# Cross-attention with two key sets: the third group's exponentials row by row

## The chip, the cores and the metric

The kernel runs on one core of a Trainium2 chip. The metric is the device time of one execution in microseconds (us). Five engines work side by side, each through its own queue in program order: TensorE (matrix products, PE in the profile, with PEld for its weight loads), VectorE (DVE), ScalarE (ACT), GpSimd (POOL) and SyncE (SP), which issues nearly all transfers between the device memory and the on-chip memory. All arithmetic is in 32-bit floats.

## The reference, cut to what matters

Two batches of 2048 tokens with 640 channels attend, with 20 heads of 32 channels, to 154 context rows of 1024 channels. The first 77 rows are text and the other 77 are a second set with its own key and value weights. There are two softmaxes per token and head, one over each set of 77 keys, and their outputs are added.

```python
def _attend(q, k, v, sm_scale):
    scores = jnp.einsum('bhsd,bhld->bhsl', q, k) * sm_scale
    probs = jax.nn.softmax(scores, axis=-1)
    return jnp.einsum('bhsl,bhld->bhsd', probs, v)
...
text = encoder_hidden_states[:, :TEXT_LEN, :]      # 77 rows
ip = encoder_hidden_states[:, TEXT_LEN:, :]        # 77 rows
q = _split_heads(hidden_states @ Wq.T, H)
k = _split_heads(text @ Wk.T, H)
v = _split_heads(text @ Wv.T, H)
out_text = _merge_heads(_attend(q, k, v, sm_scale))
k_ip = _split_heads(ip @ Wk_ip.T, H)
v_ip = _split_heads(ip @ Wv_ip.T, H)
out_ip = _merge_heads(_attend(q, k_ip, v_ip, sm_scale))
out = out_text + IP_SCALE * out_ip                 # IP_SCALE = 1
out = out @ Wo.T + bo
return out + residual
```

## The kernel before

Channels are cut into five chunks of 128, which are four heads each. A step u (0 to 19) is one batch, one chunk and one half (1024 tokens) of the sequence; `step_of` gives them. Two steps with the same batch and chunk make a pair q (0 to 9). The 1024 tokens of a step are eight tiles of 128, and `GROUPS` cuts these into three groups s of three, three and two tiles. A group holds, for each token on its partition, four heads with two rows of 77 scores per tile: 24 rows in the first and second groups, 16 rows (1232 numbers on a partition) in the third.

The order of all work is one list of words, `SCHEDULE`, written out by hand and emitted word by word. Each engine takes its own instructions in that order. The words that matter here, with s the group and u the step:

- `q.u.h@bank`: TensorE computes the queries of half h into one of eight accumulator banks (`queries`, L191); `cq.u.h`: ScalarE scales and copies them out (`take_queries`, L201).
- `Rs.u@half`: TensorE computes the scores into four banks, one for each head (`scores`, L223); `Ks.u`: ScalarE copies them to the buffer `pb` in four copies (`take`, L235).
- `Ms.u`: VectorE takes the maximum of each row (`maxima`, L261); `Ss.u`: GpSimd subtracts it, over the whole group (`subtract`, L275); `Es.u`: ScalarE takes the exponential in place, over the whole group (`exponential`, L281).
- `Ds.u`: VectorE sums the rows and takes the reciprocals (`sums`, L288 and L290); `Ns.u`: GpSimd multiplies by them (`normalise`, L295); `Ts.u`: VectorE transposes blocks of 32 x 32 (`transpose`, L302).
- `A.q@half`: TensorE multiplies both steps of a pair with the values (`attend`, L311), which needs all six transposes of the pair; `CA.q`: ScalarE copies the result out (`take_attention`, L334 and L338).
- `k` and `v` project keys and values (L132), and `ck` and `cv` are ScalarE's copies of them (L673 and L675; the first two of the keys at L548). `m`, `o` and `p` are products of the output projection, and `cm` and `co` add them up on VectorE (L467, L502, L508). `LX` loads tokens, `VS` spreads the values over partitions (L148).

After the last pair a finishing part (from L789, names `F`, `Y`, `X`, `V`) does the second batch's output projection. A word waits, through semaphores, for the words that write what it reads and for those that still read what it writes; the eight banks are used in turn, so that a product can start only when ScalarE or VectorE has emptied its bank. A function for exponentials row by row is there already (`exponential_of`), but the table `DIRECT` that selects it is empty.

Of the kernel before, what the change touches and what calls it, by code (L numbers as in the profile page):

```python
# [9 lines left out]
F32 = mybir.dt.float32  # L10
AF = mybir.ActivationFunctionType
ALU = mybir.AluOpType
AX = mybir.AxisListType

B, S, C, CC, LT = 2, 2048, 640, 1024, 154
# [5 lines left out]
def kernel(  # L21
# [25 lines left out]
    nc = tc.nc  # L47
    P = 128
    NC = C // P
    NCC = CC // P  # L50
    G = P // D
# [7 lines left out]
    L = TEXT  # L59
# [1 line left out]
    NK = (2 * L + D - 1) // D  # L61
    LP = NK * D
    SCALE = 1.0 / float(D) ** 0.5
    DIRECT = {}
    NP = B * NC
    NU = NP * SUB
    OPEN = 4
# [4 lines left out]
    small = ctx.enter_context(tc.tile_pool(name="small", bufs=4))  # L72
# [67 lines left out]
    def square_v(c):  # L140
        for b in range(B):
            nc.vector.transpose(squares(b * NC + c), vT[:, b])

    def spread_v(q, half):

        for g in range(G * half // 2, G * (half + 1) // 2):
            for r in range(G):
                nc.sync.dma_start(  # L148
                    out=v4s[q % 2][r * D : (r + 1) * D, g].rearrange("p k d -> p (k d)"),
                    in_=squares(q)[g * D : (g + 1) * D],  # L150
                )
# [28 lines left out]
    def load_wq(q):  # L180
        c = q % NC
        nc.sync.dma_start(
            out=wqs[q % 3], in_=WqT[:, ts(c, P)].rearrange("(k p) o -> p k o", p=P)
        )
# [25 lines left out]
    def keys_of(u, s):  # L210
        return pb_of(u, s)[:, :, :, : 2 * L]

    def rows_of(u, s):
        return keys_of(u, s).rearrange("p n g (t l) -> p (n g) t l", l=L)

    def scores(u, s, ps):

        _, b, c, _ = step_of(u)
        first, n = GROUPS[s]
        for t in range(n):  # L220
            h, st = divmod(first + t, TB // P)
            for g in range(G):
                nc.tensor.matmul(  # L223
                    ps[g][:, ts(t, 2 * L)],
                    qTs[(u, h)][g * D : (g + 1) * D, ts(st, P)],
                    kT[g * D : (g + 1) * D, c, b].rearrange("p t l -> p (t l)"),
                    start=True,
                    stop=True,
                )

    def take(u, s, ps):

        n = GROUPS[s][1]
        for g in range(G):
            nc.scalar.copy(  # L235
                keys_of(u, s)[:, :, g], ps[g][:, : n * 2 * L].rearrange("p (n l) -> p n l", n=n)
            )
# [3 lines left out]
    def rows_in(ps, n):  # L241
        return ps[:, : n * 2 * L].rearrange("p (n t l) -> p n t l", n=n, t=2)

    def exponential_of(u, s, ps):

        n = GROUPS[s][1]
        for g in range(G):
            for t in range(n):
                for x in range(2):
                    nc.scalar.activation(  # L250
                        rows_of(u, s)[:, t * G + g, x],
                        rows_in(ps[g], n)[:, t, x],
                        AF.Exp,
                        bias=maxs[(u, s)][:, t * G + g, x : x + 1],
                    )

    def maxima(u, s, ps=None):
        n = GROUPS[s][1] * G
        mx = small.tile([P, n, 2], F32, tag=f"mx{n}", name=f"mx_{u}_{s}")
        if ps is None:  # L260
            nc.vector.tensor_reduce(mx, rows_of(u, s), AX.X, ALU.max)  # L261
        else:
            for g in range(G):
                nc.vector.tensor_reduce(
                    mx.rearrange("p (n g) t -> p g n t", g=G)[:, g],
                    rows_in(ps[g], n // G),
                    AX.X,
                    ALU.max,
                    negate=True,
                )  # L270
        maxs[(u, s)] = mx
# [11 lines left out]
    rdens = {}  # L283

    def sums(u, s):
        n = GROUPS[s][1] * G
        den = small.tile([P, n, 2], F32, tag=f"den{n}", name=f"den_{u}_{s}")
        nc.vector.tensor_reduce(den, rows_of(u, s), AX.X, ALU.add)  # L288
        rden = small.tile([P, n, 2], F32, tag=f"rden{n}", name=f"rden_{u}_{s}")
        nc.vector.reciprocal(rden, den)  # L290
        rdens[(u, s)] = rden

    def normalise(u, s):
        n = GROUPS[s][1] * G
        nc.gpsimd.tensor_tensor(  # L295
            rows_of(u, s), rows_of(u, s), rdens[(u, s)].unsqueeze(3).to_broadcast([P, n, 2, L]), ALU.mult
        )

    def transpose(u, s):
# [4 lines left out]
    def attend(q, pa):  # L304

        zones = pb[:, ds(q % 2, SUB)].rearrange("p z n g (k s) -> p (z n) g k s", k=NK)
        for k in range(NK):
            for r in range(G):
                rows = slice(r * D, (r + 1) * D)
                for g in range(G):  # L310
                    nc.tensor.matmul(  # L311
                        pa[r][g * D : (g + 1) * D, :],
                        v4s[q % 2][rows, g, k, :],
                        zones[rows, :, g, k, :],
                        start=(k == 0),
                        stop=(k == NK - 1),
                    )
# [10 lines left out]
    def take_attention(q, pa):  # L328
        b, c = divmod(q, NC)
        rows = rows_of_attention(b, c).rearrange("p i (n r s) -> p r i n s", n=NT // NH, r=G)  # L330
        for r in range(G):
            tokens = pa[r].rearrange("p (i n s) -> p i n s", i=NHB, n=NT // NH)
            if q % 2 == 0:
                nc.scalar.copy(rows[:, r], tokens)  # L334
                continue

            for sub in range(SUB):
                nc.scalar.copy(rows[:, r, ts(sub, NH)], tokens[:, ts(1 - sub, NH)])  # L338
# [204 lines left out]
    for t in range(2):  # L543

        ps = halves[t][G - 2 + t]
# [76 lines left out]
    def emit(word):  # L622
        name, _, where = word.partition("@")
        k, *args = name.split(".")
        x, y = (*(int(a) for a in args if a.isdigit()), None, None)[:2]
        i = int(k[1:]) if k[1:].isdigit() else None
        if k[0] == "R":
            at[name] = halves[int(where)]
            scores(x, i, at[name])
        elif k == "A":  # L630
            at[name] = halves[int(where)]
            attend(x, at[name])
        elif k == "CA":
            take_attention(x, at[f"A.{x}"])
        elif k == "SQ":
            square_v(x)
        elif k == "VS":
            spread_v(x, y)
        elif k == "LX":
            load_block(x, y)  # L640
        elif k == "LQ":
            load_wq(x)
        elif k == "LK":
            load_w(x)
        elif k == "LO":
            load_wo()
        elif k == "LF":
            for part in PARTS:
                fetch(0, part)
        elif k[0] in "KMSEDNT":  # L650
            ps = at[f"R{i}.{x}"]
            if k[0] == "K":
                take(x, i, ps)
            elif k[0] in "ME":
                direct = (x, i) in DIRECT
                if k[0] == "M":
                    maxima(x, i, ps if direct else None)
                elif direct:
                    exponential_of(x, i, ps)
                else:  # L660
                    exponential(x, i)
            else:
                dict(S=subtract, D=sums, N=normalise, T=transpose)[k[0]](x, i)
        elif k == "q":
            at[name] = banks[int(where)]
            queries(x, y, at[name])
        elif k == "cq":
            take_queries(x, y, at[name[1:]])
        elif k in ("k", "v"):
            at[name] = banks[int(where)]  # L670
            project_kv(4 * x + 2 * (k == "v") + y, at[name])
        elif k == "ck":
            nc.scalar.copy(kT[:, x, :, y, :], keys_in(at[name[1:]]))  # L673
        elif k == "cv":
            nc.scalar.copy(vT[:, :, ds(y * L, L)], keys_in(at[name[1:]]))  # L675
        elif k in ("o", "p"):
            at[name] = banks[int(where)]
            last_chunk(at[name], int(k == "p"), x, range(NC - (k == "p")))
        elif k == "co":
            store_last(at[name[1:]], 0, x)  # L680
        elif k[0] == "m":
            at[name] = banks[int(where)] if where else at[f"m{JOINS[i]}.{x}"]
            product(i, 0, x, at[name])
        elif k[:2] == "cm":
            take_product(int(k[2:]), 0, x, at[name[1:]])
        elif k[0] == "W":
            sum_w(i)
        elif k[0] == "G":
            sum_t(i, 0, x)
        else:  # L690
            finish(k, args, where)
# [152 lines left out]
    for word in SCHEDULE:  # L844
        emit(word)
# [32 lines left out]
```

## Time and profile before

| | us | of the span |
|---|---|---|
| median of 2 runs (509.55 and 509.91) | 509.73 | |
| span of the profiled execution, first to last instruction | 509.3 | |
| TensorE busy with products | 496.4 | 97% |
| VectorE busy | 431.5 | 85% |
| GpSimd busy | 414.3 | 81% |
| ScalarE busy | 242.8 | 48% |
| subtractions of all groups on GpSimd (L275, 60) | 175.6 | |
| exponentials of all groups on ScalarE (L281, 60) | 94.9 | |

The profile has no time for the execution other than its span, which stands 0.4 us below the median of the runs. An engine's busy time leaves out register, branch and semaphore instructions. TensorE's products overlap each other, so its busy time is from the first to the last of a stretch without a pause. In a timeline, a row gives the start, the time it took, the engine, the line in the kernel, the operation, what it writes and reads with shapes, how many alike stand in it, and in brackets how long the engine had been idle and what ended that.

### The profile page before, as it was taken

What the parts mean: (1) busy time and instruction counts of PE and PEld (TensorE: products, weight loads), DVE (VectorE), ACT (ScalarE), POOL (GpSimd) and SP (SyncE); (2) the same over time, 40 slices, a digit from 0 to 9 for tenths busy, and PEclk for the clock granted to TensorE, in tenths of its full rate; (3) what the DMA queues carried; (4) which work ended last, traced back from release to release, by engine and by line L of the source; (5) the groups of instructions that cost most, each with busy time, mean ns of one, the idle gap of its engine ahead of it and who ended that gap; (6) DMA issues with size and microseconds to landing.
All of it is one profiled execution on the core that took longest, in us unless ns stands there. A gap on an engine that the chain in (4) does not pass through costs nothing.

```text
span 509.3 us, 9862 instructions
## 1 busy us (share of the span) xinstructions
PE 496.4 (97%) x4114; PEld 292.1 (57%) x4114; DVE 431.5 (85%) x401; ACT 242.8 (48%) x423; POOL 414.3 (81%) x176
## 2 busy tenths in 40 slices
PE   9999999999989999999999999996999999999996
PEld 5657557557458556446655565553666576444442
DVE  0078989989987989977995999799299999999986
ACT  1266657577566567654636544663466453100000
POOL 0078999999997979988998899799399999468750
PEclk9999999999999999999999999997999999999999
DMA  8994050502441554577444724534914022310017
GB/s 272 357 287 134 16 136 11 142 3 71 129 148 42 157 192 141 200 238 250 146 134 146 242 62 155 210 106 134 322 30 124 27 82 64 125 62 1 21 62 268
DMA packets 67468, 69.34 MB, mean 136 GB/s; under 512 B 5472, under 2 KB 47200, under 8 KB 67424
## 3 DMA queue, kind: packets, MB, share of 16 engines
q1 hardware_dynamic: 66704, 68.00, 42.5%
q8 instruction: 32, 0.52, 0.4%
q10 hardware_dynamic: 720, 0.72, 0.4%
q14 instruction: 12, 0.10, 0.1%
HBM read 54.94 MB, written 10.49 MB: 128 GB/s over the span
## 4 chain that ended last, share of the span: by engine, by line
PE 69%; DVE 9%; DMA 8%; POOL 8%; ACT 2%; SPq 2%; issue 1%; DVEq 0%; POOLq 0%
PE bank L191 22%; PE bank L835 11%; PE bank L477 8%; PE bank L223 8%; PE bank L311 6%; PE bank L132 6%; POOL pb L275 5%; PE bank L457 4%; DMA x<-in_x_dram 3%; DVE pb L302 3%; POOL pb L295 3%; PE bank L487 2%; DVE mx L261 2%; DVE den L288 2%; DMA wo_ct<-in_L_xattn_Wo_dram 2%; DMA aT<-in_L_xattn_Wk_ip_dram 2%
## 5 line engine op out<-in xcount | busy, mean ns | idle before, releaser
L275 POOL TENSOR_TENSOR pb<-pb,mx 128x1848 f32<-128x1848 f32 (+1 forms) x60 | 175.6, 2946 | 42.4 <-DVE mx L261 42.3
L295 POOL TENSOR_TENSOR pb<-pb,rden 128x1848 f32<-128x1848 f32 (+1 forms) x60 | 175.6, 2948 | 15.4 <-DVE rden L290 15.1
L191 PE MATMUL bank<-x,wq 128*128 128x512 f32 x400 | 182.5, 606 | 4.8 <-DMA x<-in_x_dram 4.5
L261 DVE TENSOR_REDUCE mx<-pb 128x24 f32<-128x1848 f32 (+1 forms) x60 | 109.3, 1837 | 34.4 <-ACT pb L235 34.4
L191 PEld LDWEIGHTS bank<-x,wq 128*128 128x128 f32 x400 | 75.0, 193 | 92.8 <-issue 82.8
L235 ACT COPY pb<-bank 128x462 f32<-128x462 f32 (+1 forms) x240 | 101.9, 534 | 54.2 <-PE bank L223 53.6
L281 ACT ACTIVATE pb<-pb 128x1848 f32<-128x1848 f32 (+1 forms) x60 | 94.9, 1583 | 68.0 <-POOL pb L275 67.8
L288 DVE TENSOR_REDUCE den<-pb 128x24 f32<-128x1848 f32 (+1 forms) x60 | 110.2, 1836 | 16.3 <-ACT pb L281 16.3
L302 DVE STREAM_TRANSPOSE pb<-pb 128x1920 f32<-128x1920 f32 (+1 forms) x60 | 114.6, 1924 | 0.9 <-POOL pb L295 0.9
L223 PEld LDWEIGHTS bank<-kT,qT 32*128 32x128 f32 x1280 | 47.1, 185 | 27.6 <-issue 20.2
L223 PE MATMUL bank<-kT,qT 32*128 32x154 f32 x1280 | 58.8, 307 | 1.6 <-issue 1.3
L311 PE MATMUL bank<-pb,v 32*32 32x512 f32 x1600 | 55.5, 597 | 0.7 <-ACT pb L235 0.7
L132 PE MATMUL bank<-wo_ct,aT 128*128 128x154 f32 x320 | 46.8, 301 | 0.4 <-DMA aT<-in_L_xattn_Wk_ip_dram 0.3
L132 PEld LDWEIGHTS bank<-wo_ct,aT 128*128 128x128 f32 x320 | 44.3, 192 | 4.7 <-issue 3.5
L311 PEld LDWEIGHTS bank<-pb,v 32*32 32x32 f32 x1600 | 29.8, 103 | 22.3 <-issue 10.1
L201 ACT ACTIVATE qT<-bank 128x512 f32<-128x512 f32 x40 | 23.5, 599 | 29.3 <-PE bank L191 29.2
L457 PE MATMUL bank<-aT,wo_ct 128*128 128x512 f32 x80 | 36.3, 595 | 0.0
L477 PE MATMUL bank<-aT,wo_ct 128*128 128x256 f32 x128 | 32.3, 386 | 0.0
L477 PEld LDWEIGHTS bank<-aT,wo_ct 128*128 128x128 f32 x128 | 23.6, 190 | 7.6 <-issue 4.4
L502 DVE SCALAR_TENSOR_TENSOR acc<-bank,bo_sb,acc 128x256 f32<-128x256 f32 x32 | 13.6, 466 | 14.9 <-PE bank L487 14.8
L457 PEld LDWEIGHTS bank<-aT,wo_ct 128*128 128x128 f32 x80 | 15.0, 190 | 16.8 <-issue 16.4
L781 DVE TENSOR_TENSOR x<-x,bank 128x512 f32<-128x512 f32 x36 | 23.1, 678 | 1.0 <-PE bank L835 0.9
(71 smaller groups left out, 343.0 us busy)
## 6 DMA issues: line engine op xcount, KB each, us to landing
x<-in_x_dram SPq DMA_DIRECT2D x20, 1280.0 KB, 8.4
out_dram<-acc SPq DMA_DIRECT2D x20, 256.0 KB, 2.6
x<-in_x_dram SPq DMA_DIRECT2D x18, 256.0 KB, 5.4
acc<-in_x_dram SPq DMA_DIRECT2D x16, 256.0 KB, 3.7
out_dram<-x SPq DMA_DIRECT2D x15, 256.0 KB, 2.3
v<-vS SPq DMA_DIRECT2D x160, 20.0 KB, 2.6
wq<-in_L_xattn_Wq_dram SPq DMA_DIRECT2D x9, 320.0 KB, 5.3
aT<-in_L_xattn_Wk_dram SPq DMA_DIRECT2D x5, 512.0 KB, 4.5
```

Of the source, the lines that this page charges most:

```text
L132: nc.tensor.matmul(keys_in(out), loaded[n][:, k, :], cT[:, k, :, t, :], start=(k == 0), stop=(k == NCC - 1))
L191: nc.tensor.matmul(pq, wqs[q % 3][:, k, :], xs[place_of(u, h)][:, k, :], start=(k == 0), stop=(k == NC - 1),)
L223: nc.tensor.matmul(ps[g][:, ts(t, 2 * L)], qTs[(u, h)][g * D : (g + 1) * D, ts(st, P)], kT[g * D : (g + 1) * D, c, b].rearrange("p t l -> ...
L235: nc.scalar.copy(keys_of(u, s)[:, :, g], ps[g][:, : n * 2 * L].rearrange("p (n l) -> p n l", n=n))
L261: nc.vector.tensor_reduce(mx, rows_of(u, s), AX.X, ALU.max)
L275: nc.gpsimd.tensor_tensor(rows_of(u, s), rows_of(u, s), maxs[(u, s)].unsqueeze(3).to_broadcast([P, n, 2, L]), ALU.subtract)
L281: nc.scalar.activation(e, e, AF.Exp)
L288: nc.vector.tensor_reduce(den, rows_of(u, s), AX.X, ALU.add)
L295: nc.gpsimd.tensor_tensor(rows_of(u, s), rows_of(u, s), rdens[(u, s)].unsqueeze(3).to_broadcast([P, n, 2, L]), ALU.mult)
L302: nc.vector.transpose(p, p)
L311: nc.tensor.matmul(pa[r][g * D : (g + 1) * D, :], v4s[q % 2][rows, g, k, :], zones[rows, :, g, k, :], start=(k == 0), stop=(k == NK - 1),)
L477: nc.tensor.matmul(part, w_of[m][:, kp, op], t_of(m, b, i)[:, kp], start=(op == kp == 0 and m in (1, 2, 5)), stop=(op == 1 and kp == 1 and ...
```

## The change

In the third group (s = 2) of every step, GpSimd's subtraction is left out. VectorE's maximum is written negated, by an option of the same instruction. In place of one exponential over the group, ScalarE does one for each of the 16 rows, with the row's negated maximum as the bias (a number per partition, read from memory), in place in `pb`. The order of the words is the same, and the first two groups are as before. The table `MODES` selects this by the letter "r"; the other letters (accumulating the sums, reading the banks directly, dividing, sums on GpSimd) are not used by this kernel.

```diff
-    DIRECT = {}
+    MODES = {2: "r"}
...
+    def mode(u, s):
+        return MODES.get(s, "")
+
+    def exponential_by_rows(u, s, ps):
 
         n = GROUPS[s][1]
...
         for g in range(G):
             for t in range(n):
                 for x in range(2):
+                    row = rows_of(u, s)[:, t * G + g, x]
...
                     nc.scalar.activation(
-                        rows_of(u, s)[:, t * G + g, x],
-                        rows_in(ps[g], n)[:, t, x],
+                        row,
+                        rows_in(ps[g], n)[:, t, x] if "p" in mode(u, s) else row,
                         AF.Exp,
                         bias=maxs[(u, s)][:, t * G + g, x : x + 1],
+                        **more,
                     )
...
-            nc.vector.tensor_reduce(mx, rows_of(u, s), AX.X, ALU.max)
+            nc.vector.tensor_reduce(mx, rows_of(u, s), AX.X, ALU.max, negate="r" in mode(u, s))
...
+            elif k[0] == "S" and ("p" in mode(x, i) or "r" in mode(x, i)):
+                pass
             elif k[0] in "ME":
...
-                elif direct:
-                    exponential_of(x, i, ps)
+                elif "r" in mode(x, i) or "p" in mode(x, i):
+                    exponential_by_rows(x, i, ps)
                 else:
                     exponential(x, i)
```

More of the change, by code (lines that the diff above doesn't have):

```diff
@@ L242, in rows_in @@
         return ps[:, : n * 2 * L].rearrange("p (n t l) -> p n t l", n=n, t=2)
-    def exponential_of(u, s, ps):
+    def mode(u, s):
+        return MODES.get(s, "")
+    def exponential_by_rows(u, s, ps):
         n = GROUPS[s][1]
+        if "a" in mode(u, s):
+            dens[(u, s)] = small.tile([P, n * G, 2], F32, tag=f"den{n * G}", name=f"den_{u}_{s}")
         for g in range(G):
@@ L249, in exponential_of @@
                 for x in range(2):
+                    row = rows_of(u, s)[:, t * G + g, x]
+                    more = {"accum_out": dens[(u, s)][:, t * G + g, x : x + 1]} if "a" in mode(u, s) else {}
                     nc.scalar.activation(
-                        rows_of(u, s)[:, t * G + g, x],
-                        rows_in(ps[g], n)[:, t, x],
+                        row,
+                        rows_in(ps[g], n)[:, t, x] if "p" in mode(u, s) else row,
                         AF.Exp,
                         bias=maxs[(u, s)][:, t * G + g, x : x + 1],
+                        **more,
                     )
+    dens = {}
     def maxima(u, s, ps=None):
@@ L286, in sums @@
         n = GROUPS[s][1] * G
-        den = small.tile([P, n, 2], F32, tag=f"den{n}", name=f"den_{u}_{s}")
-        nc.vector.tensor_reduce(den, rows_of(u, s), AX.X, ALU.add)
+        if (u, s) in dens:
+            den = dens[(u, s)]
+        else:
+            den = small.tile([P, n, 2], F32, tag=f"den{n}", name=f"den_{u}_{s}")
+            (nc.gpsimd if "g" in mode(u, s) else nc.vector).tensor_reduce(den, rows_of(u, s), AX.X, ALU.add)
+        if "d" in mode(u, s):
+            rdens[(u, s)] = den
+            return
         rden = small.tile([P, n, 2], F32, tag=f"rden{n}", name=f"rden_{u}_{s}")
@@ L295, in normalise @@
         nc.gpsimd.tensor_tensor(
-            rows_of(u, s), rows_of(u, s), rdens[(u, s)].unsqueeze(3).to_broadcast([P, n, 2, L]), ALU.mult
+            rows_of(u, s), rows_of(u, s), rdens[(u, s)].unsqueeze(3).to_broadcast([P, n, 2, L]), ALU.divide if 'd' in mode(u, s) else ALU.mult
         )
@@ L652, in emit @@
             if k[0] == "K":
-                take(x, i, ps)
+                if "p" not in mode(x, i):
+                    take(x, i, ps)
+            elif k[0] == "S" and ("p" in mode(x, i) or "r" in mode(x, i)):
+                pass
             elif k[0] in "ME":
-                direct = (x, i) in DIRECT
                 if k[0] == "M":
-                    maxima(x, i, ps if direct else None)
-                elif direct:
-                    exponential_of(x, i, ps)
+                    maxima(x, i, ps if "p" in mode(x, i) else None)
+                elif "r" in mode(x, i) or "p" in mode(x, i):
+                    exponential_by_rows(x, i, ps)
                 else:
```

## The prediction

> **What bounds the kernel now.** I read the page's first part for shares, then the waits (who waited for whom: total, times, longest), then the timeline of each engine around the twenty third-group exponentials. Times are those of the profiled execution; its span is 509.3 us.
>
> ```profile
> PE 496.4 (97%) x4114; PEld 292.1 (57%) x4114; DVE 431.5 (85%) x401; ACT 242.8 (48%) x423; POOL 414.3 (81%) x176
> ...
> ACT pb L281 <- POOL pb L275: 67.8, 39, 5.9
> PE bank L191 <- DMA x<-in_x_dram: 4.5, 2, 3.8
> ```
>
> TensorE is busy for 496.4 of 509.3 us: only 12.9 us are left, and of these 4.5 are waits for x. So nearly every us by which the order on TensorE is held up is a us of time, and hardly any us saved on another engine can come back. The page also shows GpSimd at 81% and ScalarE at 48%; the 67.8 us for which ScalarE's exponentials waited for GpSimd's subtractions are idle time of an engine that is not the bound. What matters is the slack of each ScalarE instruction: how long after its end TensorE needs its result or the bank that it empties. All queues are in the order of the written schedule, and the change leaves that order alone.
>
> **What goes and what comes.** The changed program has 20 subtractions fewer on GpSimd, and 16 exponentials in place of one in each of the 20 third groups; the row maximum is negated inside the same reduction, which I cost at nothing (the same instruction, on an engine whose count stays; bounds 0 and 0). No DMA is added, removed or moved past another in any queue.
>
> ```profile
> L275 POOL TENSOR_TENSOR pb<-pb,mx 128x1232 f32<-128x1232 f32 x20 | 45.1, 2257 | 3.6 <-DVE mx L261 3.6
> L281 ACT ACTIVATE pb<-pb 128x1848 f32<-128x1848 f32 x40 | 70.3, 1757 | 57.7 <-POOL pb L275 57.7
> L281 ACT ACTIVATE pb<-pb 128x1232 f32<-128x1232 f32 x20 | 24.7, 1237 | 10.4 <-POOL pb L275 10.1
> L548 ACT COPY kT<-bank 128x77 f32<-128x77 f32 x4 | 0.7, 227 | 3.8 <-PE bank L132 3.8
> 20.33 0.35 ACT L548 COPY kT<-bank 128x77 f32<-128x77 f32 x2 [1.51 <-PE bank L132]
> L779 DVE SCALAR_TENSOR_TENSOR x<-x,bo_sb,bank 128x512 f32<-128x512 f32 x15 | 10.5, 739 | 0.2 <-PE bank L835 0.2
> L781 DVE TENSOR_TENSOR x<-x,bank 128x512 f32<-128x512 f32 x36 | 23.1, 678 | 1.0 <-PE bank L835 0.9
> ```
>
> GpSimd loses 20 x 2.257 = 45.1 us, 20 x 1.237 = 24.7 us of wide exponentials go, and 320 small ones come. Their price is not in the trace. The two wide exponentials give 0.52 us for 616 elements, 0.844 ns each, and 0.197 us fixed: 0.262 us for 77 elements. They have no column operand; the nearest row that has one is VectorE's, 0.739 us with the column bo_sb against 0.678 without, 0.061 us more: 0.323 us. Neighbours on ScalarE overlap (below, the exponential from 78.71 ends at 79.94, the copy behind it starts at 79.85) by 0.09 us, so I take 0.23 us a row and 16 x 0.23 + 0.1 = 3.8 us a group, 2.55 more than 1.24. Bounds: the pair of 77-column copies takes 0.35 us, 0.227 of it the second: 0.12 a row, 2.1 us a group; without any overlap 0.323 a row, 5.2 us a group. I take the value between them because the wide exponential is nearest: same function, same memory. ScalarE's total becomes 242.8 - 24.7 + 76 = 294 us, 58% of the span: the engine as a whole stays far from a bound, and the cost lies in what stands behind each group in its queue.
>
> [...]
>
> **Unit by unit.** A unit is one step u of the schedule, its third group 2.u. A third exponential no longer waits for a subtraction, only for its maximum, but it can't pass what stands ahead of it in ScalarE's queue. Units 0 to 2:
>
> ```profile
> 38.16 1.24 ACT L281 ACTIVATE pb<-pb 128x1232 f32<-128x1232 f32 x1
> 40.08 0.29 ACT L675 COPY vT<-bank 128x154 f32<-128x154 f32 x1 [0.69 <-PE bank L132]
> ...
> 39.97 1.85 PE L223 MATMUL bank<-kT,qT 32*128 32x154 f32 x48
> ...
> 43.11 4.01 DVE L261 TENSOR_REDUCE mx<-pb 128x24 f32<-128x1848 f32 x2
> 45.22 8.74 POOL L275 TENSOR_TENSOR pb<-pb,mx 128x1848 f32<-128x1848 f32 x3 [1.59 <-DVE mx L261]
> ...
> 52.00 1.74 ACT L281 ACTIVATE pb<-pb 128x1848 f32<-128x1848 f32 x1
> 54.00 1.23 ACT L281 ACTIVATE pb<-pb 128x1232 f32<-128x1232 f32 x1 [0.27 <-POOL pb L275]
> 55.79 0.60 ACT L201 ACTIVATE qT<-bank 128x512 f32<-128x512 f32 x1 [0.56 <-PE bank L191]
> ...
> 55.69 1.80 PE L223 MATMUL bank<-kT,qT 32*128 32x154 f32 x40
> ...
> 78.71 1.23 ACT L281 ACTIVATE pb<-pb 128x1232 f32<-128x1232 f32 x1
> 79.85 0.27 ACT L675 COPY vT<-bank 128x154 f32<-128x154 f32 x1
> ...
> 80.36 1.59 PE L223 MATMUL bank<-kT,qT 32*128 32x154 f32 x40
> ```
>
> Unit 0: the group runs from 38.16 to 41.95, and the copy of vT behind it ends at 42.15 and not at 40.37. It empties a bank that the second half of the 48 score matmuls from 39.97 takes, from 40.86: TensorE stops for 1.3 us. Unit 1: the sum on VectorE that waits for the group starts 2.5 us late, and so do the two maxima at 43.11, the subtraction at 45.22 and, with 2.2, the wide exponential at 52.00; the third group then runs from 55.9 to 59.65. Behind it stands the query copy of 55.79, now done at 60.15 against 56.39, 3.75 late; the scores of the row at 55.69 have no slack against it. Less the 1.3 already lost: 2.45 us. Unit 2: the copies ahead of the group end at 78.6, so the dropped subtraction gives 0.1 us; it ends at 82.4, the copy of vT from 79.85 at 82.55, and the scores of 80.36 need its bank: 2.2 us (times of unchanged units are counted from TensorE's own delay from here on).
>
> Units 3 and 6, and 5 between them:
>
> ```profile
> 89.08 1.23 ACT L281 ACTIVATE pb<-pb 128x1232 f32<-128x1232 f32 x1
> 90.66 1.75 ACT L281 ACTIVATE pb<-pb 128x1848 f32<-128x1848 f32 x1 [0.35 <-POOL pb L275]
> 92.88 0.60 ACT L201 ACTIVATE qT<-bank 128x512 f32<-128x512 f32 x1 [0.47 <-PE bank L191]
> ...
> 92.77 1.80 PE L223 MATMUL bank<-kT,qT 32*128 32x154 f32 x40
> ...
> 126.32 1.44 DVE L288 TENSOR_REDUCE den<-pb 128x16 f32<-128x1232 f32 x1
> ...
> 143.53 1.23 ACT L281 ACTIVATE pb<-pb 128x1232 f32<-128x1232 f32 x1 [0.46 <-POOL pb L275]
> 148.43 0.27 ACT L675 COPY vT<-bank 128x154 f32<-128x154 f32 x1
> 148.56 2.08 DVE L288 TENSOR_REDUCE den<-pb 128x24 f32<-128x1848 f32 x1 [1.29 <-ACT pb L281]
> ...
> 149.34 0.79 PE L223 MATMUL bank<-kT,qT 32*128 32x154 f32 x12
> ```
>
> Unit 3: 89.08 to 92.85, then the wide exponential of 90.66 (its subtraction 2.26 earlier, so it doesn't wait) to 94.5, then the query copy to 95.0 against 93.48, needed at once by the scores from 92.77: 1.5 us. Units 4 and 5 lose 0.3 each, since ScalarE's pauses behind them take most of it. But the third sum of unit 5 starts at 128.8 and not at 126.32, and VectorE has no pause of a us until 148.56, so unit 6's first maximum, subtraction and exponential come 2.2 late; the group at 143.53 then ends at 148.95 and the copy of vT at 151.8 against 148.70, wanted by the scores of 149.34: 2.45 us. This is the one place where a late VectorE carries a delay on; elsewhere TensorE is held as long as VectorE is. Sum of units 0 to 6: 10.5 us.
>
> Later, TensorE has output products to do between the scores, and the slack is larger:
>
> ```profile
> 271.77 1.23 ACT L281 ACTIVATE pb<-pb 128x1232 f32<-128x1232 f32 x1 [0.46 <-POOL pb L275]
> 272.91 2.28 ACT L338 COPY aT<-bank 128x256 f32<-128x256 f32 x8
> ...
> 333.32 1.23 ACT L281 ACTIVATE pb<-pb 128x1232 f32<-128x1232 f32 x1 [1.17 <-POOL pb L275]
> 337.10 1.75 ACT L281 ACTIVATE pb<-pb 128x1848 f32<-128x1848 f32 x1 [2.55 <-POOL pb L275]
> ...
> 378.96 1.22 ACT L281 ACTIVATE pb<-pb 128x1232 f32<-128x1232 f32 x1
> ```
>
> Unit 15 is typical: the group can start a us before 333.32, behind it ScalarE paused until 337.10, and nothing is lost; so with 7, 9, 10, 11, 13 and 14. Unit 12 ends 1.95 late, the attention copies of 272.91 empty four banks with 1.1 us of slack: 0.85. Units 16 and 17 stand close (17 at 378.96, one query copy behind 16): 3.3 us late together, most of it hidden, 0.2 through a score copy and 1.2 through VectorE into the attention of 403 us. Units 8, 18 and 19 give 0.2, 0.45 and 0.8. Sum 3.7, and with the first 10.5: 14.2 us.
>
> **The clock.** TensorE's granted clock fell to half twice in mid-kernel, each time behind a pause:
>
> ```profile
> 151.45 1.24 PE L223 MATMUL bank<-kT,qT 32*128 32x154 f32 x12 [1.32 <-issue]
> 151.40:155.20 3.80, 3.75 (x22) 3.44 (x23) 2.66 (x2) 1.89 (x4) 3.80 (x2) 0.55 0.02 4
> ...
> 350.82 7.34 PE L191 MATMUL bank<-x,wq 128*128 128x512 f32 x10 [3.85 <-DMA x<-in_x_dram]
> 349.50:356.50 7.00, 5.68 (x7) 2.52 (x8) 6.92 (x5) 2.23 (x2) 6.67 (x3) 0.51 0.11 30
> ```
>
> A pause of 1.32 us was followed by some 3.4 us at half clock (mean 0.55 in the window), one of 3.85 by 6.8 us (0.51). Half clock for 3.4 us costs 1.7 us of TensorE. Three of my pauses are over 2 us; a slowed TensorE gives ScalarE time to catch up, so I take one and a half of them: 2.5 us, between 0 and 8.
>
> [...]
>
> Sum: 509.3 + 14.2 + 2.5 = 526.0 us, and with the 0.4 by which the median of the runs (509.73) stands above the span, 526.4.
>
> **Rivals.** *The rows are cheap.* At the wide exponential's own price with overlap, 0.17 us, a group takes 2.8 us. The same walk then gives 0.3, 1.45, 1.15, 0.5 and 0.8 for units 0, 1, 2, 3 and 6, little else: 4.5 us, 514. For it: only the column keeps a row above that price. *The subtraction pays for the rows.* Subtraction and wide exponential were 2.26 + 1.24 = 3.5 us in series; if a group takes 2.1 us (0.12 a row), a sum on VectorE comes no later, only unit 1's query copy and unit 2's bank are late, by about 1.2 us together, and what GpSimd's relief can give TensorE (0.7 us before the attention at 216, 0.3 at 444) takes it back: 509.7, not slower. It decides from about 2.2 us a group down. Against it: that price is of a copy without a column or a table function. *The rows are dear.* Without overlap, at 5.2 us, each of ten places of loss grows by 1.4: 28 us and 5 of clock, 542. For it: each small instruction carries its own column read. [...]
>
> **How the numbers follow.** My forecast with prices of 3.5 to 4.5 us, 520 to 533: 0.53, of it 0.15 for the page's clock rule. Cheap rows, 511 to 520: 0.22. Subtraction pays: 0.09. Dear rows, 533 to 545: 0.16. The range 512 to 538 leaves out most of the subtraction case and the upper half of the dear one, some 0.17. Two per cent is 10.2 us, about what a measurement can tell here from no change: over 519.9 lie the forecast and the dear rows, 0.69; within 2% the other two, 0.29; under 499.5 TensorE would have to gain 10 of its 12.9 idle us, which nothing here offers: 0.02.
>
> **What would show it.** The third group's rows at 0.21 to 0.27 us start to start, and 20 subtractions gone with GpSimd near 370 us busy. TensorE's idle time up by 10 to 17 us in pauses of 1 to 2.5 us ahead of score matmuls, released by ScalarE, nearly all before 155 us; between 200 and 350 us hardly any. More half-clock windows, each behind a pause over a us. ScalarE's waits for GpSimd well under 67.8 us. I am wrong on the price if rows start every 0.17 us or less, and wrong on the mechanism if they are dear and TensorE's idle time stays at 13 us.

## The result

The changed kernel takes 531.29 us (two runs, 530.22 and 532.36) against 509.73: 1.042 times the time before, interval 1.037 to 1.047. The profiled execution has a span of 528.3 us against 509.3, 19.0 more. All times in this document are of the fast executions; one of 1008.14 us, among the ten of the run without the subtraction, is left out.

The page of the changed kernel, its first part; then who waited for whom, with total, times and longest; then the group of the new rows (busy us, mean ns of one, idle before). In the changed kernel L257 is the new row, L291 the wide exponential, L285 the subtraction, L271 the maximum and L693 the copy of vT:

```profile
PE 502.4 (95%) x4114; PEld 295.0 (56%) x4114; DVE 432.5 (82%) x401; ACT 295.1 (56%) x723; POOL 371.0 (70%) x156
...
ACT pb L291 <- POOL pb L285: 44.0, 21, 7.8
PE bank L223 <- ACT qT L201: 6.1, 6, 2.5
PE bank L191 <- DMA x<-in_x_dram: 4.8, 3, 3.8
PE bank L223 <- ACT vT L693: 4.7, 3, 2.2
...
L257 ACT ACTIVATE pb<-pb,mx 128x77 f32<-128x77 f32 x320 | 82.0, 356 | 0.8 <-DVE mx L271 0.8
```

TensorE's busy time is 6.0 us longer and its idle time 25.9 us against 12.9, 13.0 longer: together the 19.0. The new waits are of score products (L223) for ScalarE: nine waits, 10.8 us, for query copies and for copies of vT, none of which was in the list before. GpSimd is 43 us less busy, and ScalarE's wide exponentials wait 44.0 us for it; before it was 67.8, of them 57.7 in the two groups that keep their subtraction. What that is worth, the run without the subtraction tells below. ScalarE is at 295.1 us, as far from being a bound as forecast (294).

ScalarE's timeline of the changed kernel at units 0 and 1, then TensorE's (start, time, engine, line, shapes, count, idle before and what ended it):

```profile
38.35 4.10 ACT L257 ACTIVATE pb<-pb,mx 128x77 f32<-128x77 f32 x16
42.35 0.27 ACT L693 COPY vT<-bank 128x154 f32<-128x154 f32 x1
...
56.50 4.09 ACT L257 ACTIVATE pb<-pb,mx 128x77 f32<-128x77 f32 x16
60.49 0.57 ACT L201 ACTIVATE qT<-bank 128x512 f32<-128x512 f32 x1
```

```profile
40.16 1.31 PE L223 MATMUL bank<-kT,qT 32*128 32x154 f32 x26
42.67 1.06 PE L223 MATMUL bank<-kT,qT 32*128 32x154 f32 x22 [1.20 <-ACT vT L693]
...
57.60 1.06 PE L223 MATMUL bank<-kT,qT 32*128 32x154 f32 x22
61.12 1.05 PE L223 MATMUL bank<-kT,qT 32*128 32x154 f32 x18 [2.46 <-ACT qT L201]
62.09 6.25 PE L191 MATMUL bank<-x,wq 128*128 128x512 f32 x10
...
89.04 2.22 PE L223 MATMUL bank<-kT,qT 32*128 32x154 f32 x40 [2.23 <-ACT vT L693]
...
105.64 1.05 PE L223 MATMUL bank<-kT,qT 32*128 32x154 f32 x18 [1.50 <-ACT qT L201]
106.61 6.26 PE L191 MATMUL bank<-x,wq 128*128 128x512 f32 x10
...
164.56 0.53 PE L223 MATMUL bank<-kT,qT 32*128 32x154 f32 x4 [0.84 <-ACT qT L201]
166.37 1.05 PE L223 MATMUL bank<-kT,qT 32*128 32x154 f32 x20 [1.27 <-ACT vT L693]
```

Before, the 48 score products of unit 0 ran without a break from 39.97. Now they break after 26, and the rest waits for the copy of vT at 42.35, which stands behind the 16 rows. The 40 score products after unit 1's group break for 2.46 us until the query copy of 60.49 is done, those after unit 2 start 2.23 us late, those after unit 3 break for 1.50 us. The 16 rows take 4.10 us: fifteen steps and one row of 0.356, so 0.25 us from row to row.

The clock, in windows of the changed kernel (after the busy times: granted clock, share of the DMA engines, GB/s):

```profile
62.50:66.00 3.50, 3.50 (x5) 1.35 (x4) 1.91 (x1) 1.56 (x4) 3.40 (x2) 0.51 0.11 26
89.80:93.30 3.50, 3.50 (x36) 3.19 (x29) 2.76 (x6) 3.26 (x8) 0.56 (x1) 0.51 0.00 0
106.90:110.40 3.50, 3.50 (x5) 1.34 (x5) 3.47 (x4) 1.68 (x4) 2.70 (x1) 0.51 1.05 284
366.30:369.80 3.50, 2.93 (x4) 1.39 (x5) 3.50 (x3) 1.80 (x2) 1.67 (x1) 0.51 0.09 22
```

Three stretches at half clock, of 3.4 us each, begin 0.8 to 1.4 us after the ends of the pauses of units 1, 2 and 3; the ten query products behind units 1 and 3 take 6.25 us and not 4.56. The fourth follows the wait for x that was there before.

### The profile page after: what moved, and what is told of

It is laid out like the page before. It is cut to its first block, busy times and chain, and to the rows that moved or that the text cites. A ratio compares the mean times of both kernels' runs of the same rounds, so it can differ in the third digit from the quotient of the medians.

```text
span 528.3 us, 10140 instructions
## 1 busy us (share of the span) xinstructions
PE 502.4 (95%) x4114; PEld 295.0 (56%) x4114; DVE 432.5 (82%) x401; ACT 295.1 (56%) x723; POOL 371.0 (70%) x156
## 4 chain that ended last, share of the span: by engine, by line
PE 57%; ACT 14%; DVE 13%; DMA 7%; POOL 5%; SPq 2%; issue 1%; ACTq 0%; DVEq 0%; POOLq 0%
PE bank L191 19%; PE bank L853 9%; ACT pb L257 8%; PE bank L223 7%; PE bank L493 6%; PE bank L327 6%; PE bank L132 4%; DVE den L301 4%; POOL pb L285 4%; DVE pb L318 3%; PE bank L473 3%; DMA x<-in_x_dram 3%; DVE mx L271 2%; ACT pb L291 2%; DMA wo_ct<-in_L_xattn_Wo_dram 2%; PE bank L503 2%
## 5 line engine op out<-in xcount | busy, mean ns | idle before, releaser
L285 POOL TENSOR_TENSOR pb<-pb,mx 128x1848 f32<-128x1848 f32 x40 | 131.2, 3288 | 73.8 <-DVE mx L271 73.7
L271 DVE TENSOR_REDUCE mx<-pb 128x24 f32<-128x1848 f32 (+1 forms) x60 | 109.3, 1838 | 34.2 <-ACT pb L235 34.0
L291 ACT ACTIVATE pb<-pb 128x1848 f32<-128x1848 f32 x40 | 70.0, 1755 | 44.0 <-POOL pb L285 44.0
L257 ACT ACTIVATE pb<-pb,mx 128x77 f32<-128x77 f32 x320 | 82.0, 356 | 0.8 <-DVE mx L271 0.8
L223 PE MATMUL bank<-kT,qT 32*128 32x154 f32 x1280 | 61.7, 309 | 12.1 <-ACT qT L201 6.1
L223 PEld LDWEIGHTS bank<-kT,qT 32*128 32x128 f32 x1280 | 48.7, 186 | 39.8 <-issue 18.3
L132 PE MATMUL bank<-wo_ct,aT 128*128 128x154 f32 x320 | 46.6, 300 | 0.7 <-ACT aT L354 0.4
L132 PEld LDWEIGHTS bank<-wo_ct,aT 128*128 128x128 f32 x320 | 44.1, 192 | 5.0 <-issue 2.9
L327 PEld LDWEIGHTS bank<-pb,v 32*32 32x32 f32 x1600 | 31.0, 103 | 23.1 <-issue 11.1
L201 ACT ACTIVATE qT<-bank 128x512 f32<-128x512 f32 x40 | 23.5, 597 | 26.1 <-PE bank L191 25.9
```

Of the source, the lines that this page charges most:

```text
L132: nc.tensor.matmul(keys_in(out), loaded[n][:, k, :], cT[:, k, :, t, :], start=(k == 0), stop=(k == NCC - 1))
L223: nc.tensor.matmul(ps[g][:, ts(t, 2 * L)], qTs[(u, h)][g * D : (g + 1) * D, ts(st, P)], kT[g * D : (g + 1) * D, c, b].rearrange("p t l -> ...
L257: nc.scalar.activation(row, rows_in(ps[g], n)[:, t, x] if "p" in mode(u, s) else row, AF.Exp, bias=maxs[(u, s)][:, t * G + g, x : x + 1], ...
L271: nc.vector.tensor_reduce(mx, rows_of(u, s), AX.X, ALU.max, negate="r" in mode(u, s))
L285: nc.gpsimd.tensor_tensor(rows_of(u, s), rows_of(u, s), maxs[(u, s)].unsqueeze(3).to_broadcast([P, n, 2, L]), ALU.subtract)
L327: nc.tensor.matmul(pa[r][g * D : (g + 1) * D, :], v4s[q % 2][rows, g, k, :], zones[rows, :, g, k, :], start=(k == 0), stop=(k == NK - 1),)
```

## The experiments

Each ran beside the kernel before on the same chip, which took 510.7 to 510.8 us there (12 to 25 runs, 507.7 to 514.7). The theory is the prediction's: a third group costs by what stands right behind it in ScalarE's queue and how soon TensorE wants that. The main rivals: the cost goes with the work added; or the lack of the subtraction or the late sums on VectorE are a cause of their own.

**Where: the early units alone, the late units alone.**

```diff
-        return MODES.get(s, "")
+        return MODES.get(s, "") if u < 7 else ""        # second run: u >= 7
```

> Row-by-row exponentials in units 0 to 6 alone; units 7 to 19 as before the change. Theory (the cost sits where a word that TensorE needs at once stands right behind the third group in ScalarE's queue): nearly all of the loss up to the attention of unit 5 is here, 13 to 16 us over before, 523 to 526 us, with at least two half-clock windows before 115 us. Rival (the cost goes with the number of groups, as added work on ScalarE would): 7 of 20 groups, 7 to 8 us, 517 us.

> Row-by-row exponentials in units 7 to 19 alone. Theory: 4 to 7 us over before, 514 to 517 us, lost near units 12, 16, 17, 18 and 19, and nothing in units 7, 9, 10, 11, 13, 14 and 15. Rival (cost by number of groups): 13 of 20, 14 us, 524 us.

Measured: 524.56 us, ratio 1.024 (1.017 to 1.031), and 515.55, ratio 1.009 (1.006 to 1.012). Seven early groups cost 13.9 us, thirteen late ones 4.9. The cost doesn't go with the number of groups. Together the two parts make 18.8 us, where the whole change took 21.6; the profiled execution of the first has one early stretch of half clock fewer than the changed kernel's, that of unit 2, an estimated 1.7 us (3.4 us at half clock). In the trace of the second the losses fall where the walk had them, 1.2 us at unit 12, 2.1 at units 16 and 17 and 1.1 each at 18 and 19, with 1.2 more near units 8 and 9; and 1.7 are gained at unit 6, where the kernel before had half clock. The score products of the first run, at units 2 and 3:

```profile
90.11 1.59 PE L223 MATMUL bank<-kT,qT 32*128 32x154 f32 x40 [2.24 <-ACT vT L693]
...
105.09 1.05 PE L223 MATMUL bank<-kT,qT 32*128 32x154 f32 x18 [1.50 <-ACT qT L201]
```

and its clock:

```profile
62.50:66.00 3.50, 3.50 (x21) 2.15 (x18) 1.62 (x3) 2.81 (x7) 2.26 (x2) 0.52 0.13 28
88.00:94.00 6.00, 3.89 (x57) 3.73 (x58) 3.41 (x6) 5.31 (x18) 3.29 (x1) 1.00 0.00 0
106.80:110.30 3.50, 3.50 (x5) 1.35 (x4) 3.50 (x4) 1.24 (x3) 3.15 (x1) 0.51 0.92 244
```

The two pauses are those of the changed kernel to a hundredth. But behind the pause of 2.24 us the clock stayed at 1.00 here, where the changed kernel had half clock (0.51) behind 2.23: the length of the pause alone doesn't tell these two apart, and what does is not shown.

**What: the relief alone.** In the third group the subtraction goes and the wide exponential stays.

```diff
-    MODES = {2: "r"}
+    MODES = {2: "w"}        # S is skipped for this group, E is the wide one
```

> Third group: GpSimd's subtraction is left out and the one wide exponential stays, of scores without their maximum subtracted. This is GpSimd's relief alone. Theory: TensorE is the bound and GpSimd's 45 us come off its idle side, 508 to 510 us. Rival (the relief is worth something, and the rows eat it and more): 506 us or less.

Measured: 509.89 us, ratio 0.998 (0.995 to 1.001). GpSimd's 45 us are worth nothing that can be told from zero. Among this run's waits, ScalarE's exponentials of the two other groups still wait for GpSimd, 54.0 us of 57.7 before:

```profile
ACT pb L291 <- POOL pb L285: 54.0, 26, 6.0
```

**What: the column.** Sixteen rows without a bias.

```diff
-                        bias=maxs[(u, s)][:, t * G + g, x : x + 1],
```

> Third group: 16 exponentials row by row as in the changed kernel, but without the bias column (the maximum isn't subtracted at all). Theory (the column read is a third of a row's price): rows start every 0.15 to 0.18 us, a group takes 2.5 to 2.9 us, and the time is 512 to 517 us, as the walk for cheap rows gives. Rival (it is the number of instructions, not the column): rows stay at 0.25 us, 4.1 us a group, 529 to 533 us.

Measured: 513.16 us, ratio 1.004 (1.001 to 1.007).

```profile
L257 ACT ACTIVATE pb<-pb 128x77 f32<-128x77 f32 x320 | 52.4, 270 | 0.0
38.20 2.62 ACT L257 ACTIVATE pb<-pb 128x77 f32<-128x77 f32 x16
40.72 0.27 ACT L692 COPY vT<-bank 128x154 f32<-128x154 f32 x1
```

A row without a column takes 0.270 us and starts 0.157 after the one before; with it 0.356 and 0.25. Of the step from row to row the column is 0.09 us, over a third, and at 2.62 us a group the loss is 2.5 us, not 21.6. These rows don't wait for the maximum either, but that is no rival: in the changed kernel they waited for it 0.8 us in all.

**Cause: the queue alone.** The kernel before, with empty copies behind the third group's exponential of units 0 to 6 on ScalarE.

```diff
+    pad = const.tile([P, TB // 2], F32, name="pad")
...
         nc.scalar.activation(e, e, AF.Exp)
+        if s == 2 and u < 7:
+            for _ in range(11):                          # second run: 7
+                nc.scalar.copy(pad, pad)
```

> The kernel before (subtraction and wide exponential stay), with 11 copies of a scratch tile of 256 columns on ScalarE behind the third group's exponential in units 0 to 6: some 2.8 us of empty work there (the copies at 0.25 us), and no sum, subtraction or maximum waits for it. Theory (it is what stands behind the group in ScalarE's queue): most of the loss of the run with rows in units 0 to 6 alone comes back without any row, 9 to 14 us over before, 519 to 524 us; what is missing is the part that went through VectorE (unit 1's late maxima, 0.6 us or so). Rival (the late sums on VectorE, or the missing subtraction, cause the pauses): within 3 us of before.

Measured: 541.41 us, ratio 1.058 (1.052 to 1.065). The dose was wrong: the copies, each in place on the same tile, started every 0.44 us and took 4.76 us together, not 2.8. With 7:

> The kernel before with 7 copies of the scratch tile behind the third group's exponential in units 0 to 6. The run with 11 showed the copies at 0.44 us start to start, so 7 are 2.9 us, the dose that the rows add (4.1 for 1.24). Theory (what stands behind the group waits): 10 to 14 us over before, 520 to 525 us, with TensorE's pauses at the same score products as in the run with rows in units 0 to 6. Rival (sums that come late on VectorE or the subtraction that is gone are a cause of their own): under 516 us.

Measured: 522.53 us, ratio 1.024 (1.020 to 1.028), the ratio of the run with rows in units 0 to 6; 11.9 us over before, where the rows cost 13.9.

```profile
38.56 1.24 ACT L284 ACTIVATE pb<-pb 128x1232 f32<-128x1232 f32 x1
39.69 3.02 ACT L287 COPY pad<-pad 128x256 f32<-128x256 f32 x7
42.62 0.28 ACT L681 COPY vT<-bank 128x154 f32<-128x154 f32 x1
```

The sum on VectorE is released at 39.8 here, as before the change, and the subtraction is in place; the copy of vT is as late as with the rows, and the time is nearly theirs. Part of what is missing stands at unit 1, where the profiled execution loses 1.9 us and the one with early rows 2.8; the expectation puts this down to VectorE's sum and maxima, which the rows delay there, and no run shows that alone. ScalarE's queue is enough as the cause of the rest. The two other doses, 2.5 us lost over twenty groups of 2.62 us and 31 us over seven of 5.9 (exponential and larger pad), show how steep it is beyond the slack.

**Quiet places.** Rows in units 7, 9, 10, 11, 13, 14 and 15 alone.

```diff
-        return MODES.get(s, "")
+        return MODES.get(s, "") if u in (7, 9, 10, 11, 13, 14, 15) else ""
```

> Row-by-row exponentials only in units 7, 9, 10, 11, 13, 14 and 15, where the walk found slack behind the group. Theory: no loss and no gain, 508.5 to 511 us. Rival (cost by number of groups): 7 of 20, 7 us, 517 us.

Measured: 511.72 us, ratio 1.001 (0.998 to 1.005), a little over the expected range and 0.9 us over the kernel before, which lies inside the interval: the same 16 rows, at 0.25 us, cost nothing that can be told from zero where the walk had found slack, and gain nothing.

**Place against work.** All rows as in the change, with the third group's words of units 0, 1, 2, 3 and 6 moved behind the copies that TensorE waits for.

```diff
+    MOVES = (
+        "E2.0>ck.1.1 D2.0>M1.1 E2.1>K0.2 D2.1>T0.1 N2.1>N1.1 T2.1>T1.1 E2.2>E0.3 D2.2>T1.2 "
+        "E2.3>K0.4 D2.3>T2.2 N2.3>D2.3 E2.6>K0.7 D2.6>M0.7 N2.6>D2.6"
+    ).split()
```

> The changed kernel with the third group's words of units 0, 1, 2, 3 and 6 moved later in the order: the 16 exponentials stand behind the copies that TensorE waits for, with the sums (and where needed the normalisations and one transposition) moved with them. Same instructions, same work on each engine. Theory: of the 14 us lost by the attention of unit 5, 9 to 12 come back and so do the half-clock windows, 516 to 521 us. Rival (the work itself costs the time, not its place): 528 us or more.

Measured: 526.49 us, ratio 1.032 (1.025 to 1.040): 5 us come back and not 10 to 15, so neither the theory's range nor the rival's was met. The score products behind units 0 to 3 did as expected:

```profile
40.20 1.85 PE L223 MATMUL bank<-kT,qT 32*128 32x154 f32 x48
55.91 1.80 PE L223 MATMUL bank<-kT,qT 32*128 32x154 f32 x40
...
82.24 1.59 PE L223 MATMUL bank<-kT,qT 32*128 32x154 f32 x40
94.64 1.93 PE L223 MATMUL bank<-kT,qT 32*128 32x154 f32 x40
96.51 4.56 PE L191 MATMUL bank<-x,wq 128*128 128x512 f32 x10
```

None of the first three breaks, and the fourth is 0.13 us longer than before; the query product that began at 94.51 before and at 106.61 in the change begins at 96.51. But by the attention of unit 3 (q = 1), 3.2 us are lost, by unit 5 6.9, and by unit 9 15.6, in the profiled execution: unit 3's late sum stands ahead of unit 4's maximum on VectorE, and unit 6's group now stands ahead of unit 7's copies. That execution took 531.73 us, the longest of the four (the others 525.22 to 527.06), at a mean granted clock of 0.986, where the profiled execution of the kernel before had 0.990. The moved cost arrived elsewhere. So I moved units 0 to 2 only:

> As the run with moved words, but only units 0, 1 and 2 are moved; units 3 and 6 stand as in the changed kernel. Theory: units 0 to 2 lose 1 us and not 6.8, and their two half-clock windows (1.7 us each) go; unit 3 loses 1.8 and may keep its window: 521 to 524 us. Rival (a moved group only hands the delay on to the next unit, as it did in units 4 and 6 to 8 of the run before): 526 us or more.

Measured: 525.98 us, ratio 1.030 (1.027 to 1.034). That is the rival's number and not the theory's: a moved group hands its delay on. ScalarE's rows behind unit 2's moved group show how:

```profile
88.79 4.09 ACT L257 ACTIVATE pb<-pb,mx 128x77 f32<-128x77 f32 x16
92.78 0.57 ACT L201 ACTIVATE qT<-bank 128x512 f32<-128x512 f32 x1
93.26 4.09 ACT L257 ACTIVATE pb<-pb,mx 128x77 f32<-128x77 f32 x16
97.25 1.73 ACT L291 ACTIVATE pb<-pb 128x1848 f32<-128x1848 f32 x1
98.88 0.58 ACT L201 ACTIVATE qT<-bank 128x512 f32<-128x512 f32 x1
```

Unit 2's group, moved behind E0.3, ends just where unit 3's begins, and the query copy at 98.88 is late by both: TensorE's score products behind it break for 3.82 us, not 1.50, and a stretch of 6.8 us at half clock follows (granted clock 0.51 from 99 to 106 us). Up to unit 2, and with the half clock behind it, 1.9 us are lost and not 10.3; unit 3 loses 7.2 and not 3.5.

```profile
99.52 1.90 PE L223 MATMUL bank<-kT,qT 32*128 32x154 f32 x18 [3.82 <-ACT qT L201]
101.35 6.82 PE L191 MATMUL bank<-x,wq 128*128 128x512 f32 x10
```

**Dose.** Both rows of a head and tile share a maximum: 8 exponentials of 154 columns.

```diff
-                for x in range(2):
-                    row = rows_of(u, s)[:, t * G + g, x]
...
+                row = both[:, t * G + g]
+                nc.scalar.activation(row, row, AF.Exp, bias=maxs[(u, s)][:, t * G + g, 0:1])
...
+                nc.vector.tensor_reduce(mx[:, :, 0], both, AX.X, ALU.max, negate=True)
```

> A dose: the two rows of 77 of one head and tile share one maximum (over 154 scores, the same value of the softmax), so a third group takes 8 exponentials of 154 columns with a bias column in place of 16 of 77. At 0.315 us each (0.25 and 77 more columns at 0.844 ns) a group takes 2.6 us, 1.4 more than before. Theory (the price is that of the instruction, and the loss falls faster than the dose because each place has a slack): 511 to 515 us, no half-clock window before 150 us. Rival (the loss goes with ScalarE's added work, 29 of 57 us): 521 us.

Measured: 513.48 us, ratio 1.007 (1.004 to 1.010).

```profile
L256 ACT ACTIVATE pb<-pb,mx 128x154 f32<-128x154 f32 x160 | 52.4, 426 | 0.0
38.88 2.62 ACT L256 ACTIVATE pb<-pb,mx 128x154 f32<-128x154 f32 x8
```

A group takes 2.62 us, the same as 16 rows without a column, and the time is the same as theirs within 0.4 us.

> The shared maximum and the moved words of units 0, 1 and 2 together. Theory: nothing is left but unit 3 and the tail, 509 to 513 us; it can't be clearly under before, since TensorE has no idle time to give back. Rival: the moves cost more than they save at this dose, 514 us or more.

Measured: 515.86 us, ratio 1.011 (1.007 to 1.015), 2.4 more than unmoved. The theory's number is missed, and the rival's came out. At this dose the places of units 0 to 2 cost little (2.4 us, 1.1 with the moves), and unit 3 behind the moved group loses 1.2 and not 0.3, so that by unit 5 the two profiled executions stand level. The 2.3 us between them arise later: 1.8 at unit 6, where this one has a stretch of half clock and the unmoved one none (mean granted clock of the executions 0.990 and 0.993), and most of the rest near unit 9. That the moves cause this is not shown. No run is under the kernel before beyond its interval.

## Why the prediction was right

It said 526.0 us, 512 to 538, slower by over 2% with 0.69. The mechanism and its places were right, all but unit 6. How late the same score or query product starts against before, step by step in the two timelines of TensorE, beside the walk (us):

| place | walk | seen | what was missed |
|---|---|---|---|
| unit 0 | 1.3 | 1.7 | price of a row |
| unit 1 | 2.45 | 2.8 | price of a row |
| unit 2 | 2.2 | 2.3 | |
| unit 3 | 1.5 | 1.8 | price of a row |
| units 4 and 5 | 0.6 | 0.5 | |
| unit 6 | 2.45 | -0.8 | before had a pause and half clock of its own here |
| units 8 to 19 | 3.7 | 6.9 | units 16 to 19, and a break near unit 9 |
| clock, early | 2.5 | 5.0 | three windows, not one and a half |
| clock, at the wait for x at 347 | 0 | -1.4 | |
| sum | 16.7 | 18.8 | 19.0 with 0.2 at the start |

That the sum came so near is in part luck: unit 6, 3.2 us too high, and the units behind it, 3.2 too low, cancel. Of the signs that were named, one was off: between 200 and 350 us 2.2 us were lost, and not hardly any.

*The price* was 0.23 us a row, measured 0.25, and 3.8 us a group, measured 4.1. The sum of rows from two engines came close: its 0.323 us for a row with the column stands against 0.356 measured, its overlap of 0.09 against 0.11 (0.356 less the 0.25 from row to row), and its 0.061 for the column against the 0.09 by which the step grows from 0.157 to 0.25. The rival of cheap rows fell on exactly this; what it would have given at its own price, 514 for 2.8 us a group, is borne out by the run without columns, 513.16 at 2.62, and by the shared maximum, 513.48, though their losses, 2.5 and 2.8 us, are under the 4.5 of that walk. The rivals of dear rows and of a subtraction that pays for the rows are out by the same rows.

*Unit 6.* The carrying of the delay through VectorE was right (unit 6's first exponential starts 2.2 us later against TensorE), and the score products behind the attention lost 0.84 and 1.27 us in two breaks. But the kernel before had lost time at this very place, by the pause of 1.32 us and the half clock behind it (the 32 products L132 that follow took 5.66 us, and 4.48 in the changed kernel, where the clock was 1.00 from 155 to 175 us). The walk added a pause where there was one already, and the half clock that this place gave back may belong to the one profiled execution of before and not to the kernel: the run with late rows alone, up to here the kernel before, gained 1.7 us at this place.

*The tail* was undersized: 6.9 us, of them 1.2 at unit 12 (walk 0.85), 2.1 at units 16 and 17 (1.4), 1.1 each at 18 and 19 (0.45 and 0.8), and 1.4 near units 8 and 9 (0.2), where the changed kernel has a break of 0.91 us. The same break stands in runs whose units 8 and 9 have no rows (0.76 us with rows in units 0 to 6 alone, 0.86 with seven copies, 0.89 without the subtraction), so most of the 1.4 is not the price of the rows there.

*The clock* was the term I was least sure of, and its size was right by luck: early windows 5.0 where I took 2.5, less 1.4 at the wait for x and less what unit 6 gave back. With rows in the early units alone there were two early windows and not three, behind the same pauses. The 0.15 that the forecast counts for a clock rule stood for pauses that cost no clock at all; no run shows such a rule, and here half clock (0.51) followed three pauses of 1.5 to 2.5 us, for 3.4 us each.

*What lies around the span* was 0.4 us in the sum. In the runs whose own time stands beside their span it was 1.9 (524.71 for 522.8, 509.64 for 507.7), so the profiled execution of the kernel before took an estimated 511.2 us, above both of its runs on record. From the sum's 526.4 to 531.29 are 4.9 us: 2.3 in the span, these 1.5, and 1.1 by which the median stands above the lower run, which is the profiled one.

What the runs don't settle: what decides whether half clock follows a pause of 2.2 us, and what the break near unit 9 is.

## What to carry to other kernels

An engine at half load (here ScalarE, 56% of the span) can still cost the bound engine time: read, for each instruction behind the one you lengthen, how long after its end somebody wants its result or its buffer, and expect to lose only what is over that slack, and look for half clock behind the pauses (here 5.0 of the 19.0 us, behind pauses of 1.50, 2.23 and 2.46 us). Relief of an engine that nobody waits for last was worth nothing here, even 45 us of it (ratio 0.998). And where each place has a slack, the loss is not in proportion to the dose: 2.6 us a group cost 2.5 to 3 us in all, 4.1 cost 21.6; so the price of one instruction decides, and it should be looked for with the operands that it will really have. Moving the work behind what waits helps only where the next place has slack: each of the three moved orders handed part of the delay on to the next unit.

## What the runs showed that I had not expected

- A bias column was a quarter of a small exponential's time and over a third of its step: 0.356 us and 0.25 from row to row with it, 0.270 and 0.157 without.
- These copies in place on one and the same tile didn't overlap at all: seven of 256 columns took 3.02 us, 0.436 from start to start for 0.405 each, while the copies behind them, to different places, overlap by some 0.1.
- The same pause of 2.2 us of TensorE was followed by half clock (0.51) in one kernel and not (1.00) in another.
